# Layer 2's projections by halves of 64 rows on two PSUM homes, begun inside layer 1's loop

## Chip, cores and metric

The kernel runs on one core of a Trainium2 chip. The metric is the device time of one execution in microseconds. Engines are named as in the profile: PE is TensorE (PEld its weight load), DVE is VectorE, ACT is ScalarE, POOL is GpSimd, SP is the queue that issues most DMAs.

## What is computed

Four graph layers follow one another on x of 8 batches, 2048 nodes and 64 features. Each is `x = layernorm(x + layer(x, adj))`. `adj` is a 2048 x 2048 matrix whose rows hold one value where there is an edge and zero elsewhere. Cut to what matters here:

```python
# layer 1: hypergraph attention and a neighbour sum, then the norm
industry = einsum('nm,bmf->bnf', adj / deg, x @ W_ind)
g        = ...                       # attention over 64 hyperedges, through one-hot lists
pair     = stack([industry, g], axis=2)
coefs2   = softmax(tanh(pair @ fcW + fcb) @ av, axis=-1)
x = _layernorm(x + einsum('bnk,bnkf->bnf', coefs2, pair))
# layer 2
out_self      = einsum('bni,io->bno', x, weight_self)
x_neighbors   = einsum('nm,bmi->bni', adj, x)
out_neighbors = einsum('bni,io->bno', x_neighbors, weight_neighbor)
x = _layernorm(x + out_self + out_neighbors + bias)
# layer 3: one more neighbour sum with its own scale and weight, and the norm
```

The kernel computes `adj @ (x @ weight_neighbor)` in layer 2: projection first, neighbour sum after.

## The kernel before

Nodes are cut into 16 row tiles of 128; a row tile of x is 128 partitions by 512 columns (8 batches of 64 features). Everything is float32. The pattern of `adj` is kept as 0/1 masks in DRAM, 1 MB for each row tile, and the row's value is applied after the product. A neighbour sum for one row tile is 32 matmuls of 128x128 by 128x512 into one PSUM bank: 16 column tiles, each with a high part and a low remainder of the right-hand side (`times_mask`, L1286).

The stages are: the first product with the masks and layer 0 (to about 760 us), layer 1, layer 2, layer 3.

**Layer 1** (`layer1`, L509) is a loop over `NT + 3 = 19` iterations with an order written out by hand. `units(j)` makes the attention part g from one-hot lists `oh01`, `oh23` and `S`; `industry(j)` makes the neighbour sum; `mix_and_norm(j)` mixes the two and normalises. Each is a generator, and the string `turns` (L853) says which step of which row comes next in iteration t: `u` and `v` are rows t+1 and t+2, `p` and `s` are row t, `q` and `m` row t-1, `o` row t-2, `f` row t-3. `program_order` (L195) then makes PE, DVE, ACT and POOL keep that order exactly. In iteration 17 only `o` (row 15: mult, r, s, centre, sq, var) and `f` (row 14: rstd, x2) are left, in iteration 18 only `f` of row 15. The step `rstd` is an addition and a `pow` on POOL with the constant tile `mhalf` (L836); `x2` is eight ACT operations, one for each batch (L840), that write the layer's result.

PSUM has 8 banks. In layer 1 they are, in the order of the pools: `fg` (tag "g") two, `fm` (tag "m", two buffers) two, `fs` one, `fi` one, `ff` (tag "fc") two. In SBUF the pool `fl1` holds, from its start: `minus1`, `mhalf`, `oh01`, `oh23`, `S` (the last three 8 KB in each partition, as large as one mask tile), `agg_hi`, `agg_lo`, `ext`.

**Layer 2** (L1348) opens its pools after layer 1 has closed its own, in the same places: `l2` (small working tiles, among them `xT`), then `mj2` with three mask tiles; in PSUM `acc2` two banks, `tr2` two, `mm2` two. Outside `program_order` the order on each engine is the scheduler's. For each row tile (L1366): four transposes (helper, L152), a DVE copy to `xT` (L1362), then for each pair of batch pairs two matmuls of the 128 x 128 block against `w2_sb` (L1371). `w2_sb` is 128 x 256: a block-diagonal self weight and a block-diagonal neighbour weight, so that two batches stacked on the 128 rows are handled at once and half of the weights are zeros. Then ACT writes the high part u_hi (L1379), DVE the low part u_lo (L1380) and the self part into x2 (L1383), POOL adds the bias (L1384). u_hi and u_lo reuse the buffers of the right-hand side of layer 1. Then 16 neighbour sums `a2_j` follow (L1413), each with its norm and the projection of layer 3 for the row before.

Layer 0's `project` (L1091) already has the form that the change gives to layer 2: eight matmuls on 64 rows, one for each half and batch pair.

```python
for pr in range(NP):
    for h in range(2):
        rs = slice(h * 64, (h + 1) * 64)
        nc.tensor.matmul(mm[:, h, pr, :], xTs[j][rs, pr, :], wb[rs], start=True, stop=True)
```

Of the kernel before, what the change touches and what calls it, by code (L numbers as in the profile page):

```python
# [51 lines left out]
def kernel(  # L52
# [141 lines left out]
    @contextmanager  # L194
    def program_order():  # L195

        traced = nc.cur_bb.bb.instructions
        before = traced[-1]
        yield
        start = next(k for k in reversed(range(len(traced))) if traced[k] is before) + 1  # L200
        last = {}
        for ins in traced[start:]:
            if ins.engine in (
                mybir.EngineType.PE, mybir.EngineType.DVE, mybir.EngineType.Activation,
                mybir.EngineType.Pool,
            ):
# [301 lines left out]
    @with_exitstack  # L508
    def layer1(  # L509
        stack, own, wts, fcw_sb, fcb_sb, av_sb, fcg_sb, vecs, rden, hgr, aggp, agg_st, h_sb,  # L510
        i_hi, i_lo, mask_tile, times_mask,
    ):


        l1 = stack.enter_context(tc.tile_pool(name="fl1", bufs=1))

        minus1 = l1.tile([P, 1], F32, tag="minus1", name="minus1")
        nc.vector.memset(minus1, -1.0)
        mhalf = l1.tile([P, B], F32, tag="mhalf", name="mhalf")
        nc.vector.memset(mhalf, -0.5)  # L520

# [7 lines left out]
        agg_hi, agg_lo = (  # L529
            l1.tile([P, BC], F32, tag=f"agg{i}", name=f"agg_{i}") for i in range(2)  # L530
        )
        ext = l1.tile([P, 2, 2, B], F32, tag="ext", name="ext")

        with tc.tile_pool(name="fa", bufs=2) as fa:
# [234 lines left out]
        def mix_and_norm(j):  # L769
# [70 lines left out]
                nc.scalar.activation(x2[:, j, bc], r[:, bc], AF.Copy, scale=rstd[:, b:b + 1])  # L840
            yield "x2"

# [14 lines left out]
            "u.w1 m.df m.sw o.var"  # L857
        )

        def run(who, j, whats):  # L860
            for what in whats.split():
                if 0 <= j < NT:
                    got = next(who[j])
                    assert got == what, (j, got, what)

        with program_order():
            run(unit, 0, first)
            run(unit, 0, second)
            run(unit, 1, first)
            for t in range(NT + 3):  # L870
                now = {"p": (product, t), "q": (product, t - 1), "u": (unit, t + 1), "v": (unit, t + 2),
                       "s": (unit, t), "m": (mixer, t - 1), "o": (mixer, t - 2),
                       "f": (mixer, t - 3)}
                for turn_ in turns.split():
                    who, what = turn_.split(".")
                    run(*now[who], what)
        return x2


# [351 lines left out]
    def short_program(top):  # L1231
# [67 lines left out]
        with tc.tile_pool(name="l0", bufs=1) as l0, tc.tile_pool(  # L1299
# [41 lines left out]

        x2 = layer1(
            own, wts, fcw_sb, fcb_sb, av_sb, fcg_sb, vecs, rden, hgr, aggp, agg_st, h_sb, y_hi,
            y_lo, mask_tile, times_mask,
        )


        with tc.tile_pool(name="l2", bufs=2) as l2p, tc.tile_pool(  # L1348
            name="mj2", bufs=3
        ) as mjp, tc.tile_pool(name="ylo", bufs=1) as ylop, tc.tile_pool(  # L1350
            name="acc2", bufs=2, space=PSUM
        ) as ps_acc, tc.tile_pool(name="tr2", bufs=2, space=PSUM) as ps_tr, tc.tile_pool(
            name="mm2", bufs=2, space=PSUM
# [3 lines left out]
            def x_transposed(x, j, name):  # L1357
# [3 lines left out]
                xT = l2p.tile([P, NP, P], F32, tag="xT", name=f"xT_{name}")  # L1361
                nc.vector.tensor_copy(xT, tr)  # L1362
                return xT

            u_hi, u_lo = y_hi, y_lo
            for j in range(NT):  # L1366
                xT = x_transposed(x2, j, f"l2_{j}")
                for p2 in range(2):
                    mm = ps_mm.tile([P, 2, 2, P], F32, tag="mm", name=f"u_{j}_{p2}")
                    for i in range(2):  # L1370
                        nc.tensor.matmul(  # L1371
                            mm[:, i], xT[:, 2 * p2 + i, :], w2_sb, start=True, stop=True
                        )
                    cs = slice(p2 * 256, (p2 + 1) * 256)

                    def pair(t):
                        return t[:, j, cs].rearrange("p (i c) -> p i c", i=2)

                    nc.scalar.copy(r_(pair(u_hi)), mm[:, :, 1, :])  # L1379
                    nc.vector.tensor_tensor(  # L1380
                        r_(pair(u_lo)), mm[:, :, 1, :], pair(u_hi), ALU.subtract
                    )
                    nc.vector.tensor_tensor(pair(x2), mm[:, :, 0, :], pair(x2), ALU.add)  # L1383
                nc.gpsimd.tensor_tensor(  # L1384
                    b_view(x2[:, j, :]), b_view(x2[:, j, :]),
                    bias2_sb.unsqueeze(1).to_broadcast([P, B, C]), ALU.add,
                )


            v_hi = buffer(own, 0, "v_hi")  # L1390
# [22 lines left out]
            for j in range(NT):  # L1413
                a = mask_tile(mjp, j, "l2")
                acc = ps_acc.tile([P, BC], F32, tag="acc", name=f"a2_{j}")
                for mt in range(NT):
                    times_mask(acc, a, u_hi, u_lo, mt)
# [624 lines left out]
```

## Time and profile before

The time is 1384.36 us (median of 3, 1383.07 to 1384.51); the profiled span is 1383.9 us.

| stretch (us) | what runs | PE busy | DVE busy | ACT busy | POOL busy | granted PE clock |
|---|---|---|---|---|---|---|
| 1000 to 1040 | layer 1's loop | 39.3 | 32.4 | 23.3 | 22.3 | 0.96 |
| 1040 to 1080 | its end, first projections | 27.0 | 19.4 | 20.7 | 13.7 | 0.86 |
| 1080 to 1384 | layers 2 and 3 | 294.1 | 178.4 | 52.0 | 20.4 | 0.99 |

Busy times are sums of the instructions' durations. A line of the profile names source line, engine, operation, and tiles as out<-in with buffer numbers left out; "x8" is the number of instructions. A float32 matmul shows as two pieces. In the chain of waits every row is one stretch of the work that ended last, with start and duration; "issue" is time in which nothing visible was waited for. The granted clock is the share of full TensorE clock that the chip allowed.

Groups that matter here, from the table of groups between 1040 and 1130 us: the projections L1371 (128 pieces of 128x256, 33.5 us busy), the transposes tr_l (64 pieces), the DVE copies L1362 (16 of 689 ns), the ACT casts L1379 (32 of 373 ns), the DVE operations L1380 and L1383 (32 each, 421 and 415 ns), the POOL bias L1384 (16 of 1274 ns).

### The profile page before, as it was taken

How to read it: one execution, taken by the hardware profiler on the slowest of the kernel's cores; microseconds unless marked ns; L12 is line 12 of the kernel's file. 1: busy time of each engine (PE TensorE's matmuls, PEld its weight loads, DVE VectorE, ACT ScalarE, POOL GpSimd, SP SyncE). 2: the span in 40 equal slices, each digit the busy share in tenths (PEclk: the TensorE clock that was granted, in tenths of full speed). 3: DMA queues.
4: the chain of work that ended last, by engine and by line, in shares of the span. 5: the costliest groups of instructions: out<-in, count | busy, mean ns of one | idle time of the engine just before them, and what ended most of it. 6: DMA issues, size and time to landing. Idle time of an engine off the chain costs nothing.

```text
span 1383.9 us, 19824 instructions
## 1 busy us (share of the span) xinstructions
PE 1308.3 (95%) x7692; PEld 1025.6 (74%) x7692; DVE 929.7 (67%) x1658; ACT 363.8 (26%) x844; POOL 442.3 (32%) x372
## 2 busy tenths in 40 slices
PE   7999889999999999999986799999997899999997
PEld 6777678888888888888875466666665688888885
DVE  5555347787777777777672678888885666566554
ACT  3000101212222111211221346665655321111111
POOL 0000443444444444444410345665653320000000
PEclk9999989999999999999995599999999899999999
DMA  9765323333323333221603121222220223333552
GB/s 311 215 184 173 128 95 102 102 102 102 99 93 98 103 102 101 98 98 62 218 27 114 61 79 75 76 77 76 77 76 1 92 72 116 117 122 138 184 188 71
DMA packets 91047, 153.00 MB, mean 111 GB/s; under 512 B 12097, under 2 KB 55489, under 8 KB 84673
## 3 DMA queue, kind: packets, MB, share of 16 engines
q1 hardware_dynamic: 88642, 147.46, 31.7%
q10 hardware_dynamic: 2304, 4.20, 0.8%
q8 instruction: 63, 1.03, 0.3%
q14 instruction: 38, 0.31, 0.1%
HBM read 115.97 MB, written 35.66 MB: 110 GB/s over the span
## 4 chain that ended last, share of the span: by engine, by line
PE 81%; DVE 3%; issue 2%; ACT 1%; POOL 1%; POOLq 0%; ACTq 0%; DVEq 0%
PE pp L1020 24%; PE a L1288 17%; PE ind L1288 9%; PE y2p L983 9%; PE fc L798 2%; PE u L1371 2%; PE df L807 2%; PE gp L693 2%; PE try L152 1%; PE yp L1400 1%; PE aggp L1129 1%; PE trm L152 1%; PE tr_l L152 1%; DVE r L1031 1%; PE hp L1098 1%
## 5 line engine op out<-in xcount | busy, mean ns | idle before, releaser
L1031 DVE SCALAR_TENSOR_TENSOR r<-pp,emb_sb,r 128x256 f32<-128x256 f32 x512 | 247.3, 483 | 134.3 <-PE pp L1020 119.7
L1020 PE MATMUL pp<-w_sb,xT 64*128 64x256 f32 x1024 | 163.1, 391 | 11.8 <-PE hp L1098 10.3
L1020 PE MATMUL pp<-w_sb,y1T 64*128 64x256 f32 x1024 | 156.7, 378 | 0.0
L1020 PE MATMUL pp<-w_sb,y2T 64*128 64x256 f32 x1024 | 156.6, 378 | 0.0
L1020 PEld LDWEIGHTS pp<-w_sb,xT 64*128 64x128 f32 x1024 | 98.2, 187 | 34.6 <-issue 15.1
L469 PE MATMUL y1p<-x_hi,m 128*128 128x512 f32 x256 | 106.2, 415 | 7.2 <-ACT x_hi L417 7.2
L734 POOL TENSOR_TENSOR ez<-ez,coef 128x1024 f32<-128x1024 f32 x32 | 65.1, 2033 | 141.2 <-DVE ez L732 141.2
L1020 PEld LDWEIGHTS pp<-w_sb,y1T 64*128 64x128 f32 x1024 | 104.1, 188 | 7.8
L1020 PEld LDWEIGHTS pp<-w_sb,y2T 64*128 64x128 f32 x1024 | 104.1, 188 | 7.9
L1288 PE MATMUL ind<-y_hi,mj_l 128*128 128x512 f32 x256 | 106.6, 417 | 1.0 <-DVE dlt L763 0.8
L983 PE MATMUL y2p<-y_hi,msk 128*128 128x512 f32 x256 | 103.7, 405 | 0.0
L1288 PE MATMUL a<-y_hi,mj_l 128*128 128x512 f32 x256 | 102.4, 400 | 0.0
L983 PE MATMUL y2p<-y_lo,msk 128*128 128x512 f32 x256 | 101.7, 397 | 0.0
L1288 PE MATMUL a<-y_lo,mj_l 128*128 128x512 f32 x256 | 101.6, 397 | 0.0
L469 PE MATMUL y1p<-x_lo,m 128*128 128x512 f32 x256 | 101.4, 396 | 0.0
L1288 PE MATMUL ind<-y_lo,mj_l 128*128 128x512 f32 x256 | 101.1, 395 | 0.0
L1288 PE MATMUL a<-v_hi,mj_l 128*128 128x512 f32 x256 | 100.1, 392 | 0.0
L1288 PE MATMUL a<-v_lo,mj_l 128*128 128x512 f32 x256 | 100.0, 391 | 0.0
L1124 POOL TENSOR_TENSOR hs<-h,es 128x512 f32<-128x512 f32 x16 | 16.7, 1044 | 246.3 <-ACT h L1116 222.3
L935 POOL TENSOR_TENSOR ms<-msk,srow 128x1024 f32<-128x1024 f32 x32 | 77.4, 2420 | 7.5 <-DVE ms L948 5.3
L1288 PEld LDWEIGHTS ind<-y_hi,mj_l 128*128 128x128 f32 x256 | 48.6, 190 | 33.7 <-issue 19.1
L948 DVE SCALAR_TENSOR_TENSOR ms<-ms,adj 128x1024 f32<-128x1024 f32 x32 | 63.9, 1998 | 0.0
(262 smaller groups left out, 2434.3 us busy)
## 6 DMA issues: line engine op xcount, KB each, us to landing
mj_l<-mask SPq DMA_DIRECT2D x48, 1024.0 KB, 4.9
raw<-in_at SPq DMA_DIRECT2D x32, 512.0 KB, 4.8
adj<-in_at SPq DMA_DIRECT2D x64, 256.0 KB, 3.3
mask<-msk SPq DMA_DIRECT2D x32, 512.0 KB, 3.1
xraw<-in_xn SPq DMA_DIRECT2D x8, 512.0 KB, 5.4
oh<-oh SPq DMA_DIRECT2D x16, 256.0 KB, 3.4
xT<-in_xt SPq DMA_DIRECT2D x16, 256.0 KB, 2.9
xs<-in_xn SPq DMA_DIRECT2D x16, 256.0 KB, 2.6
```

The source lines that it names most:

```text
L152: nc.tensor.matmul(dst, src, ident, start=True, stop=True, is_transpose=True)
L469: nc.tensor.matmul(accs[q][jj], r_(m[:, t, jj * P:(jj + 1) * P]), r_(part[:, mt, :]), start=i + h + t == 0 and part is x_hi, stop=i == 3 a ...
L693: nc.tensor.matmul(gp[:, u, :], r_((oh01, oh23)[i][rs, cols]), r_(part[rs]), start=part is agg_hi, stop=part is agg_lo,)
L734: nc.gpsimd.tensor_tensor(by_b(ez), by_b(ez), per_b(coef, 2 * i, 2), ALU.mult)
L798: nc.tensor.matmul(fc[:, h, :], fcw_sb[rs], sT[rs], start=True, stop=True)
L807: nc.tensor.matmul(df[:, b:b + 1], th[:, b % 2, (b // 2) * P:(b // 2 + 1) * P], av_sb, start=True, stop=True,)
L935: nc.gpsimd.tensor_tensor(ms, m, srow[j].unsqueeze(1).to_broadcast([P, 8, P]), ALU.mult)
L948: nc.vector.scalar_tensor_tensor(ms, ms, 1.0, raws[j][h], op0=ALU.mult, op1=ALU.not_equal, accum_out=bad[:, 2 * j + h:2 * j + h + 1],)
L983: nc.tensor.matmul(acc, r_(msk[j, mt // 8][:, mt % 8, :]), r_(part[:, mt, :]), start=mt == 0 and part is y_hi, stop=mt == NT - 1 and part ...
L1020: nc.tensor.matmul(pp[:, h, pl, :], terms[j][name][rs, 2 * bq + pl], w_sb[rs, k, dq * 4 * C:(dq + 1) * 4 * C], start=k == 0, stop=k == K - 1,)
L1031: nc.vector.scalar_tensor_tensor(rb, ppv[:, :, dd, :], emb_sb[:, j, d:d + 1], rb, op0=ALU.mult, op1=ALU.add)
L1288: nc.tensor.matmul(acc, r_(a[:, mt, :]), r_(part[:, mt, :]), start=mt == 0 and part is hi, stop=mt == NT - 1 and part is lo,)
```

## The change

It is meant to give TensorE work while layer 1's last norms run, and to drop the multiplications by zeros. It replaces layer 2's projection loop by steps of layer 1's loop, and does four things.

1. The weight becomes 128 x 128: [neighbour | self] stacked twice, once for each half of 64 rows. A row tile takes eight matmuls on 64 rows (`layer2`), without the zeros. The transposes' results go to SBUF by ACT in place of DVE (`features2`); the two DVE operations and the ACT cast are done once for each row over 512 columns.
2. The outputs take turns on two homes of two banks, those of layer 1's tags "g" (even rows) and "fc" (odd rows); the transposes use tag "m" and the SBUF tile tag "sT" of layer 1.
3. The steps are begun in iterations 17 and 18: after each step of a valid row one row of layer 2 is issued (eight in iteration 17, two in 18), the other six follow after the loop, all in `program_order`.
4. In `fl1` the one-hots, `S` and the two agg tiles move in front of `minus1` and `mhalf`; `mj2` is opened before `l2`, so that layer 2's three mask tiles lie in the place of `oh01`, `oh23` and `S`.

```diff
+        oh01 = l1.tile([P, N], F32, tag="oh01", name="oh01")
+        oh23 = l1.tile([P, N], F32, tag="oh23", name="oh23")
+        S = l1.tile([P, NT, P], F32, tag="S", name="S")
...
         minus1 = l1.tile([P, 1], F32, tag="minus1", name="minus1")
...
+        def features2(j):
+            tr = ps_m.tile([P, BC], F32, tag="m", name=f"tr2_{j}")
+            for pr in range(NP):
+                pc = slice(pr * P, (pr + 1) * P)
+                transpose(tr[:, pc], x2[:, j, pc])
+            xT_of[j] = small("sT", f"xT2_{j}", (P, BC))
+            nc.scalar.copy(xT_of[j], tr)
+
+        def layer2(j):
+            xT = xT_of.pop(j)
+            pool, tag = ((ps_g, "g"), (ps_fc, "fc"))[j % 2]
+            mm = pool.tile([P, 2, BC], F32, tag=tag, name=f"u_{j}")
+            mm = mm.rearrange("p h (r c) -> p h r c", r=NP)
+            for pr in range(NP):
+                for h in range(2):
+                    rs = slice(h * 64, (h + 1) * 64)
+                    nc.tensor.matmul(
+                        mm[:, h, pr, :], xT[rs, pr * P:(pr + 1) * P], w2_sb[rs],
+                        start=True, stop=True,
+                    )
+            def by_half(t):
+                return t[:, j, :].rearrange("p (r h c) -> p h r c", h=2, c=C)
+            nc.scalar.copy(r_(by_half(i_hi)), mm[:, :, :, 0:C])
+            nc.vector.tensor_tensor(by_half(x2), mm[:, :, :, C:2 * C], by_half(x2), ALU.add)
+            nc.vector.tensor_tensor(
+                r_(by_half(i_lo)), mm[:, :, :, 0:C], by_half(i_hi), ALU.subtract
+            )
+            nc.gpsimd.tensor_tensor(
+                b_view(x2[:, j, :]), b_view(x2[:, j, :]),
+                bias2_sb.unsqueeze(1).to_broadcast([P, B, C]), ALU.add,
+            )
...
+        def layer2_steps():
+            features2(0)
+            for j in range(NT):
+                while j + 1 < NT and ("x2", j + 1) not in done:
+                    yield
+                if j + 1 < NT:
+                    features2(j + 1)
+                layer2(j)
+                yield
...
                     run(*now[who], what)
+                    if t > NT and 0 <= now[who][1] < NT:
+                        next(last, None)
+            for _ in last:
+                pass
...
-        w2_sb = wts.tile([P, 2, P], F32, tag="w2", name="w2_sb")
+        w2_sb = wts.tile([P, 2 * C], F32, tag="w2", name="w2_sb")
...
-            block_diag(w2_sb[:, 0, :], w2s)
-            block_diag(w2_sb[:, 1, :], w2n)
+            for h in range(2):
+                s = slice(h * 64, (h + 1) * 64)
+                nc.sync.dma_start(w2_sb[s, 0:C], w2n)
+                nc.sync.dma_start(w2_sb[s, C:2 * C], w2s)
...
-        with tc.tile_pool(name="l2", bufs=2) as l2p, tc.tile_pool(
-            name="mj2", bufs=3
-        ) as mjp, tc.tile_pool(name="ylo", bufs=1) as ylop, tc.tile_pool(
+        with tc.tile_pool(name="mj2", bufs=3) as mjp, tc.tile_pool(
+            name="l2", bufs=2
+        ) as l2p, tc.tile_pool(name="ylo", bufs=1) as ylop, tc.tile_pool(
...
-            u_hi, u_lo = y_hi, y_lo
-            for j in range(NT):
-                xT = x_transposed(x2, j, f"l2_{j}")
-                ...
```

More of the change, by code (lines that the diff above doesn't have):

```diff
@@ L510, in layer1 @@
         stack, own, wts, fcw_sb, fcb_sb, av_sb, fcg_sb, vecs, rden, hgr, aggp, agg_st, h_sb,
-        i_hi, i_lo, mask_tile, times_mask,
+        i_hi, i_lo, mask_tile, times_mask, w2_sb, bias2_sb,
     ):
         l1 = stack.enter_context(tc.tile_pool(name="fl1", bufs=1))
[L517 to L520, printed above, removed]
         oh01 = l1.tile([P, N], F32, tag="oh01", name="oh01")
@@ L531, in layer1 @@
         )
+        minus1 = l1.tile([P, 1], F32, tag="minus1", name="minus1")
+        nc.vector.memset(minus1, -1.0)
+        mhalf = l1.tile([P, B], F32, tag="mhalf", name="mhalf")
+        nc.vector.memset(mhalf, -0.5)
         ext = l1.tile([P, 2, 2, B], F32, tag="ext", name="ext")
@@ L841, in mix_and_norm @@
             yield "x2"
+        xT_of = {}
+        def features2(j):
[28 more added lines that the diff above has]
+            )
         g_of, ind_of, dlt_of = {}, {}, {}
@@ L858, in layer1 @@
         )
+        done = set()
         def run(who, j, whats):
@@ L864, in run @@
                     assert got == what, (j, got, what)
+                    done.add((what, j))
+        def layer2_steps():
[7 more added lines that the diff above has]
+                yield
+        last = layer2_steps()
         with program_order():
@@ L1343, in short_program @@
             own, wts, fcw_sb, fcb_sb, av_sb, fcg_sb, vecs, rden, hgr, aggp, agg_st, h_sb, y_hi,
-            y_lo, mask_tile, times_mask,
+            y_lo, mask_tile, times_mask, w2_sb, bias2_sb,
         )
-        with tc.tile_pool(name="l2", bufs=2) as l2p, tc.tile_pool(
-            name="mj2", bufs=3
-        ) as mjp, tc.tile_pool(name="ylo", bufs=1) as ylop, tc.tile_pool(
+        with tc.tile_pool(name="mj2", bufs=3) as mjp, tc.tile_pool(
+            name="l2", bufs=2
+        ) as l2p, tc.tile_pool(name="ylo", bufs=1) as ylop, tc.tile_pool(
             name="acc2", bufs=2, space=PSUM
@@ L1363, in x_transposed @@
                 return xT
-            u_hi, u_lo = y_hi, y_lo
-            for j in range(NT):
-                xT = x_transposed(x2, j, f"l2_{j}")
[L1368 to L1387, printed above, removed]
             v_hi = buffer(own, 0, "v_hi")
@@ L1416, in short_program @@
                 for mt in range(NT):
-                    times_mask(acc, a, u_hi, u_lo, mt)
+                    times_mask(acc, a, y_hi, y_lo, mt)
                 r = l2p.tile([P, BC], F32, tag="r", name=f"r2_{j}")
```

## Prediction

> **What bounds the kernel now.** I read the page's busy table and its slices first, then the chain of waits between 1055 and 1130 us, then the timelines of the engines there. From the page:
>
> ```profile
> PE 1308.3 (95%) x7692; PEld 1025.6 (74%) x7692; DVE 929.7 (67%) x1658; ACT 363.8 (26%) x844; POOL 442.3 (32%) x372
> PE   7999889999999999999986799999997899999997
> PEclk9999989999999999999995599999999899999999
> ```
>
> TensorE sets the end nearly everywhere. Slice 31 (1038 to 1072 us) is one of the few with a gap: the seam between layers 1 and 2. The chain there, by start and duration:
>
> ```profile
> 1062.37 1.09 PE tr_l L152 x8
> 1063.46 1.08 PE fc L798 x4
> ...
> 1069.30 1.67 POOL rstd L836
> 1070.97 3.40 issue
> ...
> 1074.74 1.68 POOL rstd L836
> 1076.44 0.70 DVE xT_l L1362
> ...
> 1077.28 5.35 PE u L1371 x12
> ...
> 1101.32 0.47 PE a L1288 x2
> 1101.78 1.73 PE u L1371 x8
> 1103.51 0.58 PE tr_l L152 x4
> ...
> 1121.46 8.66 PE a L1288 x38
> ```
>
> Layer 2's first eight transposes run at 1062.4, but their copy to SBUF waits for the last `rstd` of layer 1: the copy's tile lies where `mhalf`, an input of that `pow`, lay. So TensorE stands still from 1068.7 to 1077.3. Then a row of projections costs 0.58 (transposes) + 1.73 (eight pieces of 256 columns) = 2.31 us, with a few mask matmuls (`a`) in between. The masks of layer 2 were issued at 1078.5.
>
> The windows view (stretch, its length, busy time of PE, PEld, DVE, ACT, POOL; then granted clock, DMA share, GB/s) shows what idleness does to the clock:
>
> ```profile
> 1061.66:1065.08 3.42, 2.19 (x13) 1.16 (x12) 1.31 (x2) 2.05 (x3) 0.00 (x0) 1.00 0.00 0
> 1065.08:1068.49 3.41, 1.46 (x13) 1.46 (x14) 1.51 (x2) 3.09 (x10) 0.00 (x0) 1.00 0.01 2
> 1068.49:1071.90 3.41, 0.61 (x5) 0.53 (x4) 2.77 (x5) 1.08 (x5) 1.91 (x2) 0.53 0.00 0
> 1078.73:1082.14 3.41, 3.41 (x10) 2.48 (x9) 1.43 (x4) 0.74 (x2) 0.00 (x0) 0.50 0.74 259
> 1082.14:1085.56 3.42, 3.42 (x20) 2.87 (x19) 2.58 (x7) 0.75 (x2) 1.56 (x2) 0.97 1.01 422
> ```
>
> A stretch of 3.41 us that is 43% busy is followed by half clock, which ends after a full stretch.
>
> **What the Trainium skill says.** "TensorE: Matmul & The Clock Gate", section "What's actually happening": an idle window of about 3.4 us brings half clock, a busy one lifts it. The stretches above agree. The same page, "Part 4: PE-mode transpose": transposes do not count as busy in the same way; nothing here shows it, and it feeds a rival. "PSUM — Partial Sum Buffer", "PSUM bank collisions raise a hardware error": two engines may not be in one bank and quadrant at once, reads included, so they are ordered. The timeline agrees: the subtraction from a projection waits for the second ScalarE copy out of the same banks, which it does not read:
>
> ```profile
> 482.28 1.16 PE L1098 MATMUL hp<-wb,xT 64*128 64x128 f32 x16
> 484.01 0.59 ACT L1116 COPY h<-hp 128x512 f32<-128x512 f32 x1
> 484.64 0.69 DVE L1117 TENSOR_TENSOR ilo<-hp,ihi 128x512 fp32r<-128x512 f32 x1 [0.51 <-ACT h L1116]
> ```
>
> "TensorEngine Tiling (Array Packing)", "Gotcha 1: PSUM Pressure": row tiles write to different banks. Hence two banks for each row's output here.
>
> **The change, part by part.** For row j call T the four transposes, C the ScalarE copy to SBUF, U the projection, H the ScalarE copy of the high part, A the addition into x2, L the subtraction (both VectorE), B the bias (GpSimd).
>
> 1. *Halves of 64 rows.* Before, U has 4 matmuls on 128 rows against 256 columns, half of them zeros (1.73 us). Now 8 matmuls on 64 rows against 128 columns, the form of `hp` above: 16 pieces, 1.16 us until the reader may start, about 0.96 of TensorE's queue. T keeps 0.50 (0.44 to 0.58 in the chain). A row is 1.46 us of TensorE, not 2.31.
>
> 2. *Evacuation.* C and H are 512 wide on ScalarE: 0.59 each as `sT` and `ihi`. A and L are 0.69 each as L1117; before it was 4 times 0.42 plus a copy of 0.69. B stays 1.27. By the rule on banks A waits for H, so one home is held for 1.16 + 0.59 + 0.62 + 0.69 and three handoffs of 0.05: 3.2 us. With two homes that is 1.6 us a row, above TensorE's 1.46.
>
> 3. *Begun in iterations 17 and 18.* Only the last rows' norms remain there. All four engines keep to program order, so each step of a row stands in its queue among layer 1's tail. VectorE: A0 L0, mult(15), A1 L1, r, A2 L2, s, A3 L3, centre, A4 to L6, var(15), A7 and on; the five foreign ones are 0.69 each. ScalarE: x2(14), eight pieces of 2.0 together, before C6 and H5; the square, 0.62, before C7; x2(15), 2.0, before C10 and H9. GpSimd: rstd(14), B0 to B7, rstd(15), B8 and on. This adds a wait: rstd(15) stands behind B7, which waits for A7; behind rstd(15) hangs x2(15), behind that on ScalarE C10 and H9, and TensorE waits for C10.
>
> 4. *Masks in the one-hots' place.* The one-hots' last readers are at 1035, so the loads (4.9 us each) land before 1065 instead of being issued at 1078.5. That is hidden. The first mask product cannot start early, though: its bank is one of home "g" (the first pool of both layers), which U14 uses last. It starts after L14. Before, about 25 of its 32 matmuls had been slipped between projections; that is given up.
>
> 5. *At no cost:* the moved small tiles, the loads of w2 (four small ones as before, two memsets less, under layer 0's TensorE work).
>
> **The sum.** The queues taken in order with these durations:
>
> - The eight tr_l no longer stand before fc(15): it starts at 1062.4, not 1063.4; th1 1063.55 to 1064.6, sub to 1065.9, df from 1066.0. TensorE is idle from 1063.5 to 1066.0, so the stretch 1061.66 to 1065.08 is only some 35% busy and half clock comes one stretch earlier. df then takes 3.4 (the same 16 pieces at half clock took 3.58 at 750 us) instead of 1.69, and ends at 1069.4.
> - T0, T1, U0, T2, U1 at half clock, 1.0 and 1.9 of queue each: 1076.2. Two busy stretches lift the clock at about 1075.3.
> - U2 starts at 1076.7, U9 at 1089.9: 13.2 us for seven rows, 1.9 each, that is 1.6 and the five VectorE steps and the ScalarE pieces of layer 1 (3.3 + 2.5 us, partly in each other's shadow).
> - A7 ends at 1089.2, B7 at 1090.6, rstd(15) at 1092.5, x2(15) at 1094.6, C10 at 1095.1. U10 starts at 1095.15. TensorE, done with T11 at 1091.5, has idled 3.7 us.
> - That gap costs a second spell at half clock, about 1095.8 to 1102.6. U10 to U15 end at 1107.3 (1104.6 without it). L14 is done then: first mask product from 1107.6, 32 matmuls of 0.228 = 7.3 us, end 1114.9.
>
> Before, that product ended at 1123.1 (VectorE's reader starts at 1123.19). From there both run the same TensorE-bound work, so the difference reaches the end: 8.2 us. 1384.4 - 8.2 = 1376.
>
> **Rivals.**
>
> - *The clock does better.* If neither drop costs anything, the same queues give the first mask product at 1100.4 and an end of 1107.7: 15.4 us, 1369. With only the first drop, 1104.9 and 1112.2: 10.9 us, 1373.5. For it: the drop hangs on where the stretches fall. Against it: 2.5 and 3.7 us of idleness are over half of a stretch.
> - *The rows go slower* than 1.9 and 1.6, by 0.3 each for handoffs in a chain PE, ACT, DVE, DVE that I have too short: 16 x 0.3 = 4.8 us, 1381. For it: C and H share one queue, and C of a later row stands before H. Against it: the handoffs in the trace are 0.03 to 0.09.
> - *The clock sticks at half* (the other side). If transposes and 64-row pieces count as little activity, as the long half-clock stretch 724 to 788 with its small matmuls hints, the first mask product starts at 1117.2, runs 7.3 + 3.4 and ends at 1127.9: 4.8 us later, 1389. Against it: layer 0's 64-row work runs at full clock, and at half clock TensorE is busy without gaps.
>
> **How the numbers follow.** The main case 0.55; better clock 0.23; slower rows 0.14; sticking clock 0.08. The bounds of the unknown sizes: T of 0.44 or 0.58 (2.2 us in sixteen rows), the half clock one stretch longer (2 us). The range 1369.5 to 1381.5 leaves out the sticking clock, the far end of the better one and of the slower rows. 0.2% is 2.8 us: faster means below 1381.6. Main and better cases are all there, and half of the slower rows: 0.85. Same takes the rest of those: 0.08. Slower is the sticking clock and surprises: 0.07.
>
> **What would show it.** U groups of 16 pieces from about 1069 us at 1.6 to 1.9 us a row; A waiting for ScalarE; a TensorE gap of 3 to 4 us in front of U10, released by C10 behind x2(15); no mask matmul before U14 is read out; mask loads issued near 1035; the first `r` of layer 2 near 1115. I am wrong if mask matmuls again stand between projections, if the gap at U10 is missing, or if a half-clock stretch lasts through the projections.

## The result, and the profile after

The changed kernel takes 1376.59 us (median of 4 runs, 1376.14 to 1377.33), the kernel before 1383.8 us (median of 4). The ratio is 0.9948, with a 95% interval of 0.9931 to 0.9966: 7.2 us less, between 4.7 and 9.5. The forecast was 1376. In a few runs of a kernel the clock is lower and the time some per cent longer; the ratios leave them out, and no seam is read from the trace of e4 below, which is such a run (span 1417.9 us). The busy table and the slices of the page of after, lines 1, 2 and 3 as shown of before:

```profile
PE 1298.8 (95%) x7820; PEld 1019.8 (74%) x7820; DVE 918.8 (67%) x1610; ACT 369.9 (27%) x844; POOL 442.7 (32%) x370
PE   7999889999999999999996799999998899999997
PEclk9999999999999999999995599999999899999999
```

At this resolution nothing is to be seen but 9.5 us less of TensorE. The work is found in the seam between layers 1 and 2, so the rest of this text measures there. As **seam** I take the time from the start of `df(14)` (the last but one of layer 1's `df`, the same instruction in all kernels) to the start of VectorE's first reader of a mask product of layer 2 (the `r` that reads `a2_0`). Its two ends in the timelines, first before, then after, there with `df(15)` between them:

```profile
1056.82 1.84 PE L807 MATMUL df<-av_sb,th 128*128 128x1 f32 x16
...
1123.19 0.75 DVE L1419 SCALAR_TENSOR_TENSOR r<-a,s,x 128x512 f32<-128x512 f32 x1 [0.54 <-PE a L1288]
```

```profile
1056.14 1.84 PE L808 MATMUL df<-av_sb,th 128*128 128x1 f32 x16
...
1066.35 3.58 PE L808 MATMUL df<-av_sb,th 128*128 128x1 f32 x16 [2.51 <-DVE th L804]
...
1114.47 0.75 DVE L1455 SCALAR_TENSOR_TENSOR r<-a,s,x 128x512 f32<-128x512 f32 x1 [6.30 <-issue]
```

Before, that is 66.4 us, after 58.3. The seam is 8.0 us shorter. From that reader to the end of the span it is 260.7 us before and 259.8 after, and between 259.8 and 260.7 in every kernel below whose trace is used: behind the seam nothing changes. What varies is the start: `df(14)` begins anywhere from 1054.4 to 1060.2 us in kernels whose program is the same up to there, so a single execution's span says less about a change of the seam than the seam itself. "Half clock" is a granted clock of 0.50.

The chain of waits of after through the seam (start, duration, what):

```profile
1069.92 1.81 PE tr L152 x8
1071.73 2.03 PE u L864 x16
1073.79 0.59 ACT y_hi L872
...
1075.69 1.30 DVE dlt L816
...
1089.57 1.28 POOL x L877
...
1091.13 1.68 POOL rstd L837
...
1093.09 1.76 ACT x L841 x7
1094.85 0.48 ACT xT L852
1095.37 2.08 PE u L864 x16
...
1106.86 14.77 PE a L1348 x64
```

Three things replace the old wait for `xT_l`. The first projections run from 1071.7 on, at half clock (2.03 us where full clock takes 1.18). The rows then go through ACT and DVE, and one of layer 1's own DVE steps (the piece `dlt`, that is mult(15)) stands in the chain with 1.30 us. Near 1090 the chain goes through the bias of row 7, `rstd(15)`, x2(15) and the copy C10 to U10: the wait that the prediction added. TensorE's timeline has it as one number, and shows in the same view what the undisturbed rows cost:

```profile
1088.64 1.16 PE L864 MATMUL u<-w_sb,xT 64*128 64x128 f32 x16
1089.73 0.66 PE L152 MATMUL tr<-ident,x 128*128 128x128 f32 x4
1090.32 1.16 PE L864 MATMUL u<-w_sb,xT 64*128 64x128 f32 x16
1091.41 0.66 PE L152 MATMUL tr<-ident,x 128*128 128x128 f32 x4
1095.37 2.08 PE L864 MATMUL u<-w_sb,xT 64*128 64x128 f32 x16 [3.31 <-ACT xT L852]
```

From start to start a projection takes 1.09 us of TensorE's queue and a row's transposes 0.59: 1.68 a row. In front of U10 TensorE stands still for 3.31 us.

The windows view of after (stretch, its length, busy time of PE, PEld, DVE, ACT, POOL; granted clock, DMA share, GB/s):

```profile
1061.67:1065.08 3.41, 1.13 (x4) 0.30 (x4) 0.67 (x2) 2.12 (x3) 0.00 (x0) 0.90 0.00 0
1065.08:1068.49 3.41, 2.14 (x10) 2.15 (x11) 1.90 (x2) 2.40 (x9) 0.20 (x1) 0.50 0.01 2
1071.91:1075.32 3.41, 3.41 (x30) 2.88 (x32) 0.91 (x2) 1.50 (x3) 0.14 (x1) 0.60 0.00 0
1092.39:1095.80 3.41, 0.43 (x4) 0.43 (x6) 0.00 (x0) 2.96 (x11) 1.64 (x2) 0.90 0.54 163
1095.80:1099.21 3.41, 3.41 (x32) 2.85 (x32) 2.38 (x4) 1.66 (x4) 1.59 (x2) 0.60 1.02 428
```

A mean of 0.90 in a stretch of 3.41 us is 0.7 us at half clock, one of 0.60 is 2.7 us. So the first spell at half clock lasts from about 1064.4 to 1074.6 (10.2 us) and the second from about 1095.1 to 1098.5 (3.4 us).

In these traces the clock changes on a fixed grid: in after, all edges of half-clock spells between 1000 and 1100 us (1026.82, 1030.23, 1064.36, 1074.60, 1095.08, 1098.50) lie whole multiples of 3.413 us apart. Where the grid lies against the program differs between traces: its first edge after the start of `df(14)` comes 0.6 to 0.7 us later in e1, e3, e7 and e9, and 1.3 to 1.7 us later in before, after and the others whose traces are used. This will matter below.

Two more lines are not as forecast. The first masks of layer 2 are issued at 1092.83 us, not near 1035, and the table of waits of the SP queue (the queue that issues the loads) names what the load waited for (releaser, total, times, longest):

```profile
SPq L1343 <- POOL rstd L837: 58.4, 1, 58.4
```

And three of layer 1's last VectorE steps take twice their usual time. DVE and POOL of after:

```profile
1075.61 1.38 DVE L816 SCALAR_TENSOR_TENSOR dlt<-sw,dlt 128x512 f32<-128x512 f32 x1
1078.12 1.38 DVE L820 SCALAR_TENSOR_TENSOR r<-dlt,r 128x512 f32<-128x512 f32 x1
1080.62 0.67 DVE L823 TENSOR_REDUCE s<-r 128x8 f32<-128x512 f32 x1
1082.41 1.37 DVE L825 SCALAR_TENSOR_TENSOR r<-s,r 128x512 f32<-128x512 f32 x1
```

```profile
1075.18 1.27 POOL L877 TENSOR_TENSOR x<-x,bias_sb 128x512 f32<-128x512 f32 x1 [4.90 <-DVE x L873]
1077.68 1.27 POOL L877 TENSOR_TENSOR x<-x,bias_sb 128x512 f32<-128x512 f32 x1 [1.23 <-DVE x L873]
```

Each of the slow ones (1.38 in place of 0.69) begins some 0.44 us after a bias addition of GpSimd has begun and ends 0.55 us after it has ended: mult ends at 1076.99, the addition at 1076.45. The reduction `s` began in the middle of such an addition too, and took its 0.67.

### The profile page after: what moved, and what is told of

Read it like the earlier page. It is cut to its first block, busy times and chain, and to the rows that moved or that the text cites. A ratio compares the mean times of both kernels' runs of the same rounds, so it can differ in the third digit from the quotient of the medians.

```text
span 1374.3 us, 19988 instructions
## 1 busy us (share of the span) xinstructions
PE 1298.8 (95%) x7820; PEld 1019.8 (74%) x7820; DVE 918.8 (67%) x1610; ACT 369.9 (27%) x844; POOL 442.7 (32%) x370
## 4 chain that ended last, share of the span: by engine, by line
PE 90%; DVE 4%; issue 2%; ACT 2%; POOL 1%; DMA 1%; SPq 0%; ACTq 0%; POOLq 0%; DVEq 0%
PE pp L1077 24%; PE a L1348 17%; PE ind L1348 9%; PE y2p L1040 9%; PE y1p L469 9%; PE fc L799 3%; PE df L808 2%; PE gp L694 2%; PE try L152 1%; PE aggp L1186 1%; PE trm L152 1%; PE yp L1436 1%; DVE r L1088 1%; PE hp L1155 1%; PE red L744 1%
## 5 line engine op out<-in xcount | busy, mean ns | idle before, releaser
L1077 PE MATMUL pp<-w_sb,xT 64*128 64x256 f32 x1024 | 162.8, 390 | 11.7 <-PE hp L1155 10.3
```

Of the source, the lines that this page charges most:

```text
L1077: nc.tensor.matmul(pp[:, h, pl, :], terms[j][name][rs, 2 * bq + pl], w_sb[rs, k, dq * 4 * C:(dq + 1) * 4 * C], start=k == 0, stop=k == K - 1,)
```

## The experiments

All seams and times in one table; each kernel's edit and what follows are below. Seams come from one trace each, times are medians with the ratio to the kernel before that ran beside them. That kernel took 1383.8 us beside the change and 1385.5 to 1385.9 beside the experiments, so times from different rows can be compared to about 2 us only.

| kernel | seam, us | time, us | ratio (95%) |
|---|---|---|---|
| before | 66.4 | 1383.8 | |
| the change | 58.3 | 1376.59 | 0.9948 (0.9931 to 0.9966) |
| e1, all rows after the loop | 60.6 | 1379.66 | 0.9954 (0.9938 to 0.9971) |
| e2, late bias | 54.3 | 1371.2 | 0.9902 (0.988 to 0.9924) |
| e3, full rows | 66.3 | 1382.63 | 0.9988 (0.9972 to 1.0004) |
| e4, old places | | 1384.15 | 0.9982 (0.9964 to 1.0001) |
| e5, small tiles first | 58.4 | 1376.29 | 0.9929 (0.9912 to 0.9945) |
| e6, working tiles ahead of masks | 64.8 | 1383.9 | 0.9988 (0.997 to 1.0007) |
| e7, late bias and row 0 early | 51.3 | 1370.53 | 0.9888 (0.9871 to 0.9904) |
| e8, row 0 early | 55.2 | 1373.08 | 0.992 (0.9898 to 0.9942) |
| e9, late bias and dense filling | 50.8 | 1370.47 | 0.9892 (0.9875 to 0.9908) |
| e10, late bias and thin filling | 55.0 | 1373.78 | 0.9919 (0.9898 to 0.9941) |
| e11, as e7 with dense filling | 55.0 | 1372.27 | 0.9911 (0.9894 to 0.9929) |
| e12, the change with dense filling | 56.6 | 1374.15 | 0.9917 (0.9903 to 0.9932) |

### Which part of the change carries it: e1, e3, e4

e1 takes the start inside the loop away and leaves all else:

```diff
-                    if t > NT and 0 <= now[who][1] < NT:
+                    if t > NT + 2 and 0 <= now[who][1] < NT:
                         next(last, None)
```

> All sixteen rows of layer 2 are issued after the loop, behind row 15's norm on every queue; all else as in the changed kernel. Theory (cheap rows bring the gain; the start in the loop is paid back by the stall of row 15's norm): the copy C0 waits for x2(15) until about 1078 us, but no gap comes before U10; rows of 1.6 us, first reader of layer 2 at 1113 to 1116 us against 1114.5 in the changed kernel, so 1377 us, between 1375 and 1379. Rival (the early start brings the gain): the 8 us are lost again, about 1384 us.

It took 1379.66 us, a little above the 1375 to 1379 expected and far from the rival's 1384; the seam is 60.6. TensorE's timeline of e1:

```profile
1059.58 1.84 PE L808 MATMUL df<-av_sb,th 128*128 128x1 f32 x16
...
1071.29 3.57 PE L808 MATMUL df<-av_sb,th 128*128 128x1 f32 x16 [2.51 <-DVE th L804]
...
1084.20 2.08 PE L864 MATMUL u<-w_sb,xT 64*128 64x128 f32 x16 [7.53 <-ACT xT L852]
...
1087.26 1.27 PE L864 MATMUL u<-w_sb,xT 64*128 64x128 f32 x16
...
1089.05 1.16 PE L864 MATMUL u<-w_sb,xT 64*128 64x128 f32 x16
```

One gap of 7.53 us, then rows without another up to U15 (0.42 us), the later ones at 1.68 us. The seam is 2.3 us longer than the change's. But 1.5 of these 2.3 us have passed before the edit acts: up to `df(15)` the programs are the same, and `df(15)` starts 11.7 us after `df(14)` here and 10.2 in the change, because the clock, on its other grid, falls 4.1 us after `df(14)` and not 8.2. From `df(15)` to the reader e1 takes 48.9 us and the change 48.1. So what the early start saves by these traces is 0.8 us, and the two ratios, 0.9954 and 0.9948, don't tell the kernels apart. It does not save the 7.5 of the gap: the change pays for it with slower rows, a gap of its own of 3.3 us and the second spell at half clock. e1 also shows what sets the pace when nothing disturbs: between two casts ACT waits 0.46 us for PE, and PE for nobody. TensorE is the bound, not the evacuation.

e3 puts the multiplication by zeros back (128 rows, 256 columns, block-diagonal weights) and leaves all else:

```diff
-            for pr in range(NP):
-                for h in range(2):
-                    rs = slice(h * 64, (h + 1) * 64)
-                    nc.tensor.matmul(mm[:, h, pr, :], xT[rs, pr * P:(pr + 1) * P], w2_sb[rs], ...)
+            for pr in range(NP):
+                nc.tensor.matmul(
+                    mm[:, pr // 2, (pr % 2) * 2 * P:(pr % 2 + 1) * 2 * P],
+                    xT[:, pr * P:(pr + 1) * P], w2_sb, ...)
```

> The projections go back to four matmuls on 128 rows against the block-diagonal weight of 256 columns; two banks and two homes, the 512-wide evacuations and the start in the loop stay. Theory (halves of 64 rows are worth about 0.7 us of TensorE for each of sixteen rows, partly hidden under the evacuation): first reader of layer 2 at 1119 to 1121 us, the time 1382 us, between 1380 and 1384. Rival (the early start brings the gain, the rows' length is hidden by the evacuations): 1377 us.

It took 1382.63 us. Two projections in its TensorE timeline give the row, with the transposes between them left out:

```profile
1094.30 1.89 PE L861 MATMUL u<-w_sb,xT 128*128 128x256 f32 x8
...
1096.47 1.89 PE L861 MATMUL u<-w_sb,xT 128*128 128x256 f32 x8
```

2.17 us from row to row, 0.49 more than 1.68; sixteen rows make 7.8 us. The seam is 8.0 us longer, but as in e1 the grid of the clock gives 1.5 of them ahead of the edit (`df(15)` starts 11.7 us after `df(14)`). From `df(15)` to the reader e3 takes 6.5 us more than the change. Without the halves little or nothing of the change's gain is left: the ratio is 0.9988, with an interval that reaches 1.

e4 puts all tiles and pools in their old places:

```diff
-        oh01, oh23, S, agg_hi, agg_lo, minus1, mhalf      (order in fl1)
+        minus1, mhalf, oh01, oh23, S, agg_hi, agg_lo
...
-        with tc.tile_pool(name="mj2", bufs=3) as mjp, tc.tile_pool(name="l2", bufs=2) as l2p, ...
+        with tc.tile_pool(name="l2", bufs=2) as l2p, tc.tile_pool(name="mj2", bufs=3) as mjp, ...
```

> The order of the small tiles in layer 1's pool and of layer 2's pools is put back as in the kernel before; all else as in the changed kernel. Theory (the places bring nothing: the mask loads are issued only after row 15's rstd either way, and the first mask product starts after U14's evacuation): 1376.6 us, within 1 us; masks issued at 1093 to 1097 us. Rival (the masks' place is needed for the early first product): 3 to 8 us slower, 1380 to 1385 us.

It took 1384.15 us, so my theory that places cost nothing fell and its rival held. e5 and e6 split it.

### What the places do: e5, e6

e5 puts back only the order of tiles in `fl1`, e6 only the order of the two pools; together their diffs are that of e4.

> Layer 1's small tiles (minus1, mhalf) and the one-hots stand again in the order of the kernel before; the mask tiles of layer 2 are still opened ahead of the small working tiles. My theory: what layer 2's masks wait for is whole pools of layer 1, those they lie over, not single tiles; they still lie over the same pool, so nothing changes: 1376.5 us (1375.5 to 1378), masks issued near 1093 us, as after. Rival: the place of mhalf decides (its last reader is the last rstd): then the time goes to that of the run with both old places, 1382 to 1385, and the masks are issued near 1143.

> Only the order of the pools is put back: small working tiles of layer 2 first, mask tiles behind them; the order of tiles inside layer 1's pool stays as changed. My theory: the mask tiles now reach over a pool of layer 1 whose tile holds the transposed rows until the last projection, so the loads wait for U15: first mask product some 6 to 8 us later, 1383 us (1381 to 1385). Rival: the order of pools is without effect and the place of mhalf decides: 1376.6.

e5 is the change again (1376.29 us, seam 58.4, masks issued at 1093.36). e6 is e4 again (1383.9 us, seam 64.8). The table of waits of the SP queue of e6, and then its chain:

```profile
SPq L1343 <- PE u L864: 80.4, 1, 80.4
```

```profile
1106.21 1.18 PE u L864 x16
...
1107.52 4.72 DMA mj_l<-mask
...
1112.38 12.75 PE a L1348 x46
```

With the small tiles in front, the three mask tiles reach over a place of layer 1 that U15 still reads (`sT`, which now holds layer 2's transposed rows), and the first load, 4.72 us, lies bare between U15 and the first mask product. With the masks in front they lie inside `fl1`, which is done with `rstd(15)`. Both wait lists name one thing, the last user of a whole pool: moving `mhalf`, the tile that `rstd(15)` reads, from the masks' place (e5 against the change) altered nothing. So the one-hots' last readers at 1035 never mattered. In the kernel before, the same old places had no such price, because there the last user was x2(15), not a projection; the load left at 1078.53:

```profile
SPq L1283 <- ACT x L840: 13.9, 1, 13.9
```

So the new order of the pools averts a wait that the change itself would bring by putting the transposed rows into `sT`.

### What holds up U10: e2

e2 keeps the first eight bias additions back until `rstd(15)` is on its way:

```diff
+            owed.append(j)
+            if ("rstd", NT - 1) in done:
+                add_biases()          # all of owed, in order
-            nc.gpsimd.tensor_tensor(b_view(x2[:, j, :]), b_view(x2[:, j, :]), bias2..., ALU.add)
```

> The bias additions of rows 0 to 7 stand behind rstd(15) on GpSimd, not before it; all else as in the changed kernel. Theory (x2(15) is late because rstd(15) stands behind eight bias additions): rstd(15) ends 1.9 us earlier, the gap before U10 falls from 4.0 to about 2 us, the second spell at half clock goes; the first reader of layer 2 is at 1110.5 to 1112.5 us, the time 1373.5 us, between 1372 and 1375. Rival (GpSimd is not on the path; the gap comes from VectorE's late var(15) alone): no change, 1376.6 us.

1371.2 us, a larger gain than expected (1372 to 1375), and below both kernels. U10 and the DVE steps of layer 1 in e2:

```profile
1091.35 1.16 PE L864 MATMUL u<-w_sb,xT 64*128 64x128 f32 x16 [1.48 <-ACT xT L852]
```

```profile
1074.49 0.68 DVE L816 SCALAR_TENSOR_TENSOR dlt<-sw,dlt 128x512 f32<-128x512 f32 x1
1076.62 0.68 DVE L820 SCALAR_TENSOR_TENSOR r<-dlt,r 128x512 f32<-128x512 f32 x1
1080.21 0.68 DVE L825 SCALAR_TENSOR_TENSOR r<-s,r 128x512 f32<-128x512 f32 x1
```

Counted from `df(14)`, U9 starts 1.1 us earlier than in the change (33.1 against 34.2), U10 2.9 us earlier (36.3 against 39.2) and the reader 4.1 us earlier. So 1.1 us comes from VectorE's steps, 0.68 again without GpSimd beside them; 1.8 from the shorter gap; 1.2 from the second half clock, which is gone: U10 takes 1.16 us. The 1.48 that are left come from x2(15), eight ScalarE pieces of 2.0 us that begin when `rstd(15)` ends and stand in front of C10.

### What lowers the clock: e7 to e12

The prediction had read the half clock as following from a stretch in which TensorE is busy for less than half. e7 and e8 fill that stretch: row 0's transposes, copy, projection and evacuation, and row 1's transposes and copy, are begun one iteration earlier, between the steps of row 15 (e7 with the late bias, e8 without it).

```diff
+        early = {
+            "m.tr1": lambda: transposes2(0),
+            "m.th0": lambda: features2_tail(0),
+            "m.fc1": lambda: (transposes2(1), project2(0)),
+            "m.th1": lambda: (features2_tail(1), evacuate2(0, low=False)),
+            "m.sub": lambda: evacuate2(0, high=False),
+        }
...
                     run(*now[who], what)
+                    if t == NT and turn_ in early:
+                        early[turn_]()
```

> The bias additions of rows 0 to 7 behind the last rstd, and besides, row 0's transposes, copy, projection and evacuation and row 1's transposes begun one iteration earlier, where TensorE has nothing between fc(14), fc(15) and df(15). My theory: the half clock of 1063 to 1073 us comes from those idle 4 us (a stretch 31 to 35% busy); with 1.1 + 1.2 us more of work in it TensorE stays at full clock, df(15) takes 1.7 instead of 3.6, and rows 1 to 9 stand about 5 us earlier than with the late bias alone: 1366 us (1363.5 to 1368.5). Rival: the drop comes anyway (work in small matmuls does not count, or the idle stretch only moves): 1370 to 1372, as with the late bias alone.

> Row 0 and row 1's transposes begun one iteration earlier, but the bias additions where the change has them. My theory: two separate losses, each with its own spell of half clock. The first goes (as above), the gap of some 3.3 us before U10 and the second spell stay: 1372 us (1370 to 1374). Rival: the losses are one (what is won at the first is waited for at rstd(15), behind the bias additions): 1375.5 to 1377.

e7 took 1370.53 us, e8 1373.08: both seams are 3 us shorter than without the early row, though for e7 against e2 the grid differs. But the expected 1366 of e7 is missed, and half clock came all the same: in e8 one stretch later than in the change (1066.9 to 1073.7), in e7 from 1060.9 to 1067.7 and again from 1071.2 to 1074.6. The windows view of e8, for the 3.41 us that end where the clock falls, and of e2 for the same:

```profile
1063.49:1066.90 3.41, 2.58 (x30) 2.39 (x30) 2.42 (x3) 3.40 (x11) 0.90 (x1) 1.00 0.01 2
```

```profile
1059.90:1063.31 3.41, 1.13 (x4) 0.30 (x4) 1.27 (x2) 2.09 (x3) 0.00 (x0) 1.00 0.03 5
```

33% busy before the fall in e2, 76% in e8. What fills e8's stretch is U0, 64-row matmuls, and `df`, whose moving side is one column wide. Layer 1's loop has the same without any edit: in after, TensorE is busy for 3.41 of the 3.41 us from 934.66 to 938.07, `df` among the work, and the next stretch, 938.07 to 941.48, has half clock. So a second theory: work that uses little of the array doesn't hold the clock. e9 and e10 test it with fillers of about one length but of two kinds, 20 matmuls in the same three idle places, on top of e2:

```diff
+        def fill(n):                       # e9: dense
+            o = ps_g.tile([P, 2, BC], F32, tag="g", name=f"fill_{n}")
+            for _ in range(n):
+                nc.tensor.matmul(o[:, 0, :], r_(i_hi[:, NT - 1, 0:P]), r_(i_lo[:, NT - 1, :]), ...)
+        fills = {"m.tr0": 3, "m.tr1": 7, "m.fc1": 10}
...
+                nc.tensor.matmul(o[:, 0, 0:1], w2_sb, av_sb, ...)      # e10: thin, in its place
...
+                    if t == NT and turn_ in fills:
+                        fill(fills[turn_])
```

> The late bias additions, and 20 matmuls more that compute nothing that is used: the form of the mask products (128x128 by 128x512), 3 behind the transposes of g(15), 7 behind those of ind(15), 10 behind fc(15), in stretches where TensorE stood still for 0.8, 1.7 and 2.5 us. My theory, formed from the runs with row 0 begun early, where the clock fell although no stretch was less than 60% busy: what holds the clock up is work on the whole array; df (128x1), transposes and the 64-row fc count little. Then these matmuls keep full clock, df(15) takes 1.8 us instead of 3.6 and the first rows 1.7 instead of 3: 1367 us (1365.5 to 1368.5), first mask product near 1097. Rival: the drop has another cause (a time grid, power): 1371 to 1373, as without them or a little worse.

> The same places and numbers, but each added matmul is of df's form (128x128 by 128x1, two pieces of 0.11 us, about as long in TensorE's queue as one of 128x512). My theory: TensorE is as busy by the record, but hardly any of its array is, so half clock comes as with the late bias alone and lasts as long or longer: 1371 to 1374. Rival: being busy by the record is what counts: 1367, like the dense ones.

The two windows views over the same two stretches, counted from `df(14)` (4.9 to 8.3 us and 8.3 to 11.7 us after its start); first e9, then e10:

```profile
1065.05:1068.46 3.41, 3.32 (x14) 1.84 (x14) 1.27 (x2) 2.09 (x3) 0.00 (x0) 1.00 0.00 0
1068.46:1071.87 3.41, 3.41 (x23) 2.72 (x21) 1.55 (x2) 3.05 (x10) 0.00 (x0) 1.00 0.01 2
```

```profile
1059.49:1062.90 3.41, 3.18 (x24) 2.33 (x23) 1.24 (x2) 2.12 (x3) 0.00 (x0) 1.00 0.00 0
1062.90:1066.31 3.41, 3.41 (x19) 3.41 (x18) 1.58 (x2) 3.02 (x10) 0.00 (x0) 0.50 0.01 2
```

By the record TensorE is nearly as busy in e10 (93 and 100%) as in e9 (97 and 100%). With the dense fillers the clock stays at 1.00; with the thin ones it falls at 1062.9 and stays down for 10.2 us, as in e2. The seams say the same: 50.8 and 55.0, against 54.3 without filler. So do the times, beside the same runs of the kernel before: 1370.47 and 1373.78 us.

The pair alone leaves a rival: the grid. The stretches shown are steps of e10's grid; e9's first edge comes 0.66 us after `df(14)`, not 1.52. Other traces answer it. e1 and e3 have e9's grid (0.64 and 0.66) and no filler, and their clock falls 4.1 us after `df(14)`; e12 below has the dense filler on a grid near e10's (1.28), and it doesn't fall there. What it is in the thin filler that doesn't hold the clock is not separated: each of its matmuls moves one column, shows as two pieces where a dense one shows as one, and so loads weights twice (weight loads fill all 3.41 us of e10's second stretch, and 2.72 in e9).

Against e2 the dense filler shows less in time: 1370.47 us, where 1365.5 to 1368.5 was expected, against 1371.2; the seam promised 3.4. The traced execution of e9 was the longest of its four (1373.45) and reached `df(14)` at 1060.16, 5.1 us later than that of e2: its clock was 0.90 between 800 and 850 us, where e2 has 0.98. That accounts for this one execution (1371.5 + 5.1 - 3.4 = 1373.2). The three others, 1370.1 to 1370.7, have no trace; why they are not near 1368 is open.

e11 joins e7 with 10 dense fillers, e12 puts e9's fillers into the change as it is:

```diff
-        fills = {"m.tr0": 3, "m.tr1": 7, "m.fc1": 10}
+        fills = {"m.tr0": 3, "m.tr1": 4, "m.fc1": 3}       # e11, behind the early steps
```

> Row 0 begun one iteration earlier and late bias additions, with 10 of the 128x512 matmuls that compute nothing used (3 behind the transposes of g(15), 4 behind row 0's, 3 behind U0). My theory: full clock through fc(15), df(15) and the first rows; row 0 is done before df(15) ends, so about 2 us better than the dense matmuls with the late bias alone: 1365.5 us (1363.5 to 1367.5). Rival: 10 are too few among so many transposes and 64-row pieces, the clock drops at U0 or df: 1369 to 1371, as without them.

> The change as it is (bias additions where it has them), with the same 20 matmuls of 128x512 that compute nothing used, in the same three idle places. Measured by the seam from the start of df(14) to the first reader of a mask product in layer 2, 58.3 us in the change: my theory is that the first spell of half clock costs the change some 3.5 us by itself, and the second, behind the gap before U10, stays: seam 54.8 us (54.2 to 55.6), time 1373 us (1371.5 to 1374.5). Rival: the rows wait for the evacuation (VectorE beside GpSimd) and for rstd(15) anyway, so a clock held up is waited away: seam 57.5 to 58.5, 1376 to 1377.

e11 is no test of the clock. Its three last fillers write the home that U0 had just filled, so they waited for L0, a gap of 2.12 us that the edit itself made; the clock fell right behind it, and 1372.27 us misses both theories; its seam is 3.7 us longer than e7's.

e12 took 1374.15 us with a seam of 56.6, between the two theories (54.8, and 57.5 to 58.5). Its first spell is gone, as the theory had it, and U10 starts 36.1 us after `df(14)`, 3.1 earlier than in the change. Then the second spell lasts longer (6.8 us in place of 3.4), by the windows of e12:

```profile
1092.39:1095.80 3.41, 2.95 (x20) 2.50 (x20) 1.49 (x3) 1.96 (x4) 1.27 (x1) 0.50 0.83 327
1095.80:1099.21 3.41, 3.41 (x25) 2.75 (x26) 1.65 (x3) 1.26 (x3) 1.27 (x1) 0.54 0.99 382
```

It gives 1.4 of the 3.1 us back. The first spell costs the change about 3 us at U10, and what of it can be had depends on the gap behind.

## Why the prediction was right, point by point

- **The sum.** 8.2 us were predicted between the first readers; the seam shortened by 8.0, the time by 7.2. The working held to a few tenths where it could be checked: A7 ended at 1089.5 (1089.2 predicted), B7 at 1090.9 (1090.6), `rstd(15)` at 1092.8 (1092.5), U10 began at 1095.37 (1095.15), the reader at 1114.47 (end of the product at 1114.9). That is not all merit: U2 to U9 took 13.9 us where 13.2 were forecast, and the second spell cost 1.2 where 2.7 were. That such errors nearly cancel is luck.
- **Step 1, the halves: mechanism right, size off.** T was put at 0.50 and measured 0.59, U at 0.96 and measured 1.09; TensorE's row is 1.68 us, not 1.46. e3 shows the halves worth some 6.5 us of seam.
- **Step 2, the evacuation.** A does wait for H (every A of the timeline that waits is released by `y_hi`). But the two homes don't set the pace. They hold back only U3 and U15 (0.22 and 0.42 us, for L); in the undisturbed rows TensorE's 1.68 lies above the 1.6 of the evacuation, and e1 shows ACT waiting for PE. The wrong engine, an error of 0.08 a row.
- **Step 3, begun inside the loop: right in its mechanism, and it is the part of least worth (0.8 us by e1, not told from nothing by the times).** The gap before U10 (3.31, predicted 3.7), its cause, GpSimd's order, and its second half clock were forecast, and e2 takes them away by the order alone. But the five foreign VectorE steps were put at 0.69 each; three of them took 1.38 beside the bias additions (1.37 the last). The Trainium skill's page "SBUF — State Buffer", section "Who interferes with whom", says it: a VectorE instruction with two SBUF inputs contends with a GpSimd instruction that reads SBUF, the shared port is an exclusive lock, and the order of issue decides which of the two waits. The traces agree: mult, r and centre have two SBUF inputs, start after GpSimd's addition and end 0.55 us after it, 1.38 against 0.68 in e2; the reductions (one input), A and L (one side in PSUM) keep 0.67 to 0.69. I had not looked for it. In time it is small: from U2 to U9 a row takes 1.99 us, where 1.9 was predicted, and 1.84 in e2.
- **Step 4, the masks: "hidden" was right, the reason wrong.** The loads don't leave at 1035 but at 1092.83, behind the last user of the whole pool, and are hidden because the first product begins at 1106.85. That the product waits for the last projections and gives up the interleaved matmuls came as said, except that it waited for H15, the last high part (1106.85), and not for L14 (1106.60).
- **Step 5, "at no cost": right for the small tiles (e5), and blind to the pools.** The order of the pools, taken as a detail of step 4, decides 6.5 us of seam and some 7 of time (e6): without it the first load stands bare and half clock follows. The remark on the kernel before, that its copy waited because its tile lay where `mhalf` lay, is open to the same doubt: in e5 the place of `mhalf` is without effect on the masks, which wait for the whole pool. No run moved the copy's own tile.
- **The clock: times right, cause too simple.** Half clock came one stretch earlier, as forecast, and lifted at 1074.6 (predicted 1075.3). The second spell was put at 6.8 us with a cost of 2.7; it lasted 3.4 and cost 1.2. But that a stretch busy for less than half is what brings it isn't the rule: it came behind stretches busy for 76% (e8), 93% (e10) and 100% (layer 1's loop) too. The page "TensorE: Matmul & The Clock Gate", section "What's actually happening", speaks of idle and busy windows; "Part 4: PE-mode transpose" says that transposes don't count as busy in the same way. No run here tests transposes by themselves; what e9, e10 and e12 add is that matmuls with one moving column, busy by the record, did not hold the clock. The rival of the sticking clock had a mechanism of this kind, but named the wrong work: rows of transposes and 64-row projections did lift the clock after one to two full stretches, and held it.

The parts of the change don't add up. Taking away the halves, the places or the early start costs 6.5, 6.5 and 0.8 us of seam, 13.8 together, while the whole change brings 8.0. The places avert a loss that the change itself would bring, and the change gives up the mask matmuls that stood between the old projections; how much each of the two explains was not measured.

Two kernels beat both: e2, 1371.2 us, and e7, 1370.53 us with a ratio of 0.9888 (0.9871 to 0.9904), whose interval lies below that of the change. e7 adds no work to the change, only another order.

## What to carry to other kernels

When a stage is moved under the tail of another, write down for every in-order engine what then stands in front of the tail's last link: here eight additions that nobody was waiting for stood ahead of the one `pow` on which everything hung, and moving them shortened the seam by 4.1 us where the whole change had brought 8.0. A buffer's place is worth looking up even when its transfer seems hidden, because the wait can be on the last user of a whole region. And don't judge by its busy share alone whether TensorE will keep its clock: look at what keeps it busy, here how many matmuls of one column stand in the stretch. A seam compared between two single traces needs a look at where the clock's grid lies in each; here it alone made 1.5 us.

## What the runs showed of the hardware that I had not expected

- Twenty matmuls of 128x1 kept TensorE 93% busy by the record and did not keep its clock; twenty of 128x512 in the same places, of about the same length, did (e10, e9, and e12 on a grid near e10's). A stretch of layer 1's loop busy for 100% was followed by half clock.
- Three VectorE steps with two SBUF operands took 1.38 us beside a GpSimd addition and 0.68 without it, while the addition kept its 1.27.
- Programs that are the same up to `df(14)` reached it up to 5.8 us apart (1054.4 to 1060.2); in the one case followed up (e9 against e2), through more half clock between 800 and 850 us.
- The clock's grid of 3.413 us lay up to 1.1 us apart against `df(14)` in these traces (0.64 to 1.65), and on the earlier grid the same program reached `df(15)` 1.5 us later (e1 and e3 against the change).
